# A graph network on one core: the constant rows' matmuls on all 128 partitions instead of three

## The chip, the cores and the metric

The kernel runs on one core of one Trainium2 chip. The metric is the device time of one execution in microseconds; the median of three runs is given. Beside it stands one execution taken by the hardware profiler, from which all the rows and timelines below come. PE is the matmul engine (PEld is its weight load), DVE, ACT and POOL are the vector, scalar and GpSimd engines, SP issues DMAs.

## The reference

Sixteen graphs of 1024 nodes with 128 features each, and a symmetric 0/1 adjacency with ones on the diagonal. A first layer is attention over the neighbours, a second one is three GraphSAGE layers on an adjacency from which some edges are taken first (`_dilate`), and each has a residual. Cut to what matters here:

```
def _sage(x, adj, Wr, Wx, b, mf):
    agg = jnp.einsum('bij,bjd->bid', adj, x) / deg
    out = agg @ Wr + x @ Wx + b
    nrm = jnp.maximum(jnp.linalg.norm(out, axis=-1, keepdims=True), NORM_EPS)
    return out / nrm * mf[..., None]
def _bn(x, g, b):
    ...
    return (x - m) * jax.lax.rsqrt(v + BN_EPS) * g + b
h1 = _bn(jax.nn.relu(_sage(x, adj_d, Wr1, Wx1, b1, mf)), g1, be1)
h2 = _bn(jax.nn.relu(_sage(h1, adj_d, Wr2, Wx2, b2, mf)), g2, be2)
h3 = _bn(jax.nn.relu(_sage(h2, adj_d, Wr3, Wx3, b3, mf)), g3, be3)
xc = jnp.concatenate([h1, h2, h3], axis=-1) * mf[..., None]
return (xc @ Wl + bl) * mf[..., None]
```

The bias `b` of a layer, and what the batch norm of the layer before adds to every node once it is folded into the next weights, are the same row of 128 numbers for all nodes: the constant rows of the title.

## The kernel before

The program has a fast path (`fast`) and a general one behind a flag; the fast path is what runs. It sorts every graph's nodes so that those with many neighbours stand first, and then works in stages, one graph ("batch" below, 16 of them) after the other:

- Attention with the search for the edges to be taken, to about 785 us. It holds no constant row.
- Layer 1, about 790 to 922 us. Per batch, `mix` makes one SAGE product, `turn` transposes the result of the batch before, and beside them run the last part of the edge search (`dil.solve`), the transposes of later batches (`enter`) and the last stores.
- Layer 2, 930 to 1016 us: `mix` and `turn` alone, no DMA.
- Layer 3, 1022 to 1152 us: `mix`, `turn`, and `thirds`, which multiplies the outputs of layers 1 and 2 with their parts of Wl. Results of 11 of the 16 batches are scattered back to the original order of nodes through `y_d` in DRAM and loaded again.
- The final stage, 1162 to 1221 us: `raised` transposes the rows that came back, `final_half` multiplies with the last third of Wl, and the output leaves, for 11 batches by one DMA of SP each, for the other five (`STAY`) by eight scatters of POOL each.

`fast` runs with a manual schedule: each engine executes its instructions in the order in which the program records them. `in_turn` takes one piece at a time of the named generators (a tick), and `clock.later(n, ...)` puts an eviction off by n ticks. In layer 2 the order of a batch is mix, mix, mix, turn, mix, turn: the product with wr and its row; half 1 with wx and its row; half 0 and its row; the transposes of the first half of the batch before; the product with the adjacency; the transposes of the second half. In layer 3 the order is mix, thirds, mix, mix, turn, mix, thirds, turn.

What stands around the matmuls of this change: ACT squares a half (L984) when its row is in, DVE sums the squares (L987), takes the maximum (L1009), ACT the root (L1010), DVE the reciprocal (L1013) and scales both halves (`scale`, L1016). `turn` (L1026) transposes the scaled rows on PE, ACT takes the relu (L1038), DVE the batch norm's sums (L1035). `add` (L1043) is DVE's sum of a PSUM tile and a tile in SBUF. `evict` (L957, L958) is ACT's copy of wr's product, which comes from L946. wx's matmuls are L970, the adjacency's L1006 and L1007, those of `thirds` L1194 and L1195, of `final_half` L1251, and `raised` transposes in L1237.

In layer 3 and after, `pace_scatters` lets POOL issue a scatter (L547) in two of three ticks. Ahead of each, in layer 3, POOL copies a `mark` (L1169) from the newest result of DVE, so that it can't run ahead. A `y` tile has three buffers, so a batch waits for the scatters of an earlier one.

A constant row is added inside the accumulation in PSUM. `pieces` (L615 on) splits the f32 row into three bf16 pieces whose sum is the row, one per partition, and repeats them four times along the free axis; `ones3`, three partitions of 128 ones, is the stationary operand, so that a matmul with three partitions adds the three pieces to all 128 nodes of a tile. These matmuls are:

- `row_of_ph` (L950): 256 columns, 16 times each in layers 2 and 3.
- `row_of` (L975): 512 columns, twice per batch in all three layers, 96 in all.
- in `final` (L1259): 512 columns, 32 times.

In the first batch of layers 2 and 3 (`bias_last`) the three rows come at the end, one after the other, since the row is not ready before.

```
nc.tensor.matmul(halves[g].rearrange("p a b -> p (a b)"), ones3, bias, start=False, stop=(g == 1))
```

Of the kernel before, what the change touches and what calls it, by code (L numbers as in the profile page):

```python
# [8 lines left out]
BF = mybir.dt.bfloat16  # L9
# [6 lines left out]
P = 128  # L16
# [503 lines left out]
def fast(ctx: ExitStack, tc: tile.TileContext, a, out, vp):  # L520
    nc = tc.nc
# [3 lines left out]
    consts = ctx.enter_context(tc.tile_pool(name="consts", bufs=1))  # L525
# [7 lines left out]
    nc.vector.tensor_scalar(identf, jp, 0.0, None, op0=OP.is_equal)  # L533
    eps = consts.tile([P, 1], F32, name="eps")
    nc.vector.memset(eps, EPS)
    ones3 = consts.tile([3, P], BF, name="ones3")
    nc.vector.memset(ones3, 1.0)

    def apart(d, own, *others):

# [71 lines left out]
        while gens:  # L612
            gens = [g for g in gens if _advance(g)]

    def pieces(name, rows, pool):  # L615

        n = len(rows)
        v = pool.tile([3, 2, P], F32, name="pcv", bufs=1)[:, :n]
        part = pool.tile([3, 2, P], BF, name="pcp", bufs=1)[:, :n]
        acc = pool.tile([3, 2, P], F32, name="pca", bufs=1)[:, :n]  # L620
        res = pool.tile([3, n, 4, P], BF, name=name, bufs=1)
        for i, (base, more) in enumerate(rows):
            if base is None:
                nc.vector.tensor_copy(v[:, i, :], more)
            elif more is None:
                nc.vector.tensor_copy(v[:, i, :], base)
            else:
                nc.vector.tensor_add(v[:, i, :], base, more)
        for i in range(3):
            nc.vector.tensor_copy(part, v)  # L630
            if i == 0:
                nc.vector.tensor_scalar(acc, part, identf[:3, i:i + 1], None, op0=OP.mult)
            else:
                nc.vector.scalar_tensor_tensor(acc, part, identf[:3, i:i + 1], acc, op0=OP.mult, op1=OP.add)
            if i < 2:
                nc.vector.tensor_sub(v, v, part)
        nc.vector.tensor_copy(res, acc[:, :, None, :].to_broadcast([3, n, 4, P]))
        return [res[:, i].rearrange("p a b -> p (a b)") for i in range(n)]


    late = ExitStack()
# [5 lines left out]
    rows = ExitStack()  # L647
    with ExitStack() as s1:
# [206 lines left out]
        for i in range(B):  # L855
# [6 lines left out]
            if i == 0:  # L862
# [5 lines left out]
                bs = [rows3(f"b3_{k}", a[f"L1_gnn_b{k}"]) for k in (1, 2, 3)]  # L868
# [23 lines left out]

            return hT, parts()

        bias0, = pieces("pc0", [(bs[0], None)], work)
        ENTER = NB // 2
        H = {}
        for t in range(22):
# [3 lines left out]
            b = t // 4 - 1  # L902
# [36 lines left out]
    def mix(b, hT, wxk, wrk, bias, rbias, ob, on_scalar=False):  # L939

        bias_last = rbias is not None and b == 0
        ph = ps.tile([P, 2, P], F32, name="ph", bufs=ph_bufs)
        for s in range(2):
            nc.tensor.matmul(ph[:, s, :], hT[:, s * P:(s + 1) * P], wrk, start=(s == 0),  # L946
                             stop=(rbias is None and s == 1))

        def row_of_ph():
            nc.tensor.matmul(ph.rearrange("p a b -> p (a b)"), ones3, rbias[:, :2 * P], start=False, stop=True)  # L950

        if rbias is not None and not bias_last:
            row_of_ph()
        hr = work.tile([P, 2, P], F32, name="hr")

        def evict():
            nc.scalar.activation(hr[:, 0, :], ph[:, 0, :], AF.Copy)  # L957
            nc.scalar.activation(hr[:, 1, :], ph[:, 1, :], AF.Copy, scale=kept[:, b, 1:2])  # L958

        if not bias_last:  # L960
            later(1, evict)
            yield
        n = work.tile([P, 4, NB], F32, name="nrm")
        halves = {}

        def wx_half(g):
            po = halves[g] = ps.tile([P, 4, P], F32, name="po", bufs=4)
            for i in range(3, -1, -1):
                c = (4 * g + i) * P
                nc.tensor.matmul(po[:, i, :], hT[:, c:c + P], wxk, start=(i == 3), stop=False)  # L970
            if not bias_last:
                row_of(g)

        def row_of(g):
            nc.tensor.matmul(halves[g].rearrange("p a b -> p (a b)"), ones3, bias, start=False, stop=(g == 1))  # L975

        def squares(g):
            sq = work.tile([P, 4, P], F32, name="sq")
            if on_scalar and g == 1:
                for i in range(4):  # L980
                    later(1 + i // 2, lambda i=i: nc.scalar.activation(
                        sq[:, i, :], halves[g][:, i, :], AF.Square, accum_out=n[:, 0, 4 * g + i:4 * g + i + 1]))
                return
            later(1, lambda: nc.scalar.activation(sq, halves[g], AF.Square))  # L984

            def reduce():
                nc.vector.tensor_reduce(n[:, 0, 4 * g:4 * g + 4], sq, axis=AX.X, op=OP.add)  # L987
                last[0] = n[:, 0, 4 * g:4 * g + 1]

            later(2, reduce)  # L990

        wx_half(1)
        if bias_last:
            wx_half(0)
            row_of_ph()
            row_of(1)
            row_of(0)
            later(1, evict)
            yield
        squares(1)  # L1000
        yield
        if not bias_last:
            wx_half(0)
        yield
        po = halves[0]
        nc.tensor.matmul(po[:, 0, :], accT[:, b, :], hr[:, 0, :], start=False, stop=False)  # L1006
        nc.tensor.matmul(po[:, 1, :], identf, hr[:, 1, :], start=False, stop=True)  # L1007
        squares(0)
        later(2, lambda: nc.vector.tensor_scalar(n[:, 1], n[:, 0], NORM_EPS2, None, op0=OP.max))  # L1009
        later(3, lambda: nc.scalar.activation(n[:, 2], n[:, 1], AF.Sqrt))  # L1010

        def scale():
            nc.vector.reciprocal(n[:, 3], n[:, 2])  # L1013
            for g in (1, 0):
                c = slice(4 * g, 4 * g + 4)
                nc.vector.tensor_mul(ob[:, c, :], halves[g], n[:, 3, c, None].to_broadcast([P, 4, P]))  # L1016

        later(4, scale)
        yield
# [28 lines left out]
    def batchnorm(k, weights):  # L1048

        m = few.tile([P, 8], F32, name=f"bn{k}")  # L1050
        nc.vector.bn_aggr(m[:, 0:2], stats)
        nc.scalar.activation(m[:, 2:3], m[:, 1:2], AF.Sqrt, bias=eps)
        nc.vector.reciprocal(m[:, 3:4], m[:, 2:3])
        nc.vector.tensor_mul(m[:, 4:5], m[:, 3:4], gs[k])
        scaled = []
        for i, w in enumerate(weights):
            t = few.tile([P, P], F32, name=f"ws{i}", bufs=2)
            nc.scalar.activation(t, w, AF.Copy, scale=m[:, 4:5])
            scaled.append(t)
        nc.vector.tensor_mul(m[:, 5:6], m[:, 0:1], m[:, 4:5])  # L1060
        nc.vector.tensor_sub(m[:, 6:7], bes[k], m[:, 5:6])
        t3 = few.tile([P, 3], F32, name=f"t3_{k}")
        nc.vector.tensor_copy(t3, m[:, 6:7].to_broadcast([P, 3]))
        pr = ps.tile([3, 3, P], F32, name="ph")
        for i, w in enumerate(weights):
            nc.tensor.matmul(pr[:, i, :], t3, w, start=(i == 0), stop=(i == len(weights) - 1))
        return scaled, pr
# [62 lines left out]
    with big:  # L1130
        ps = big.enter_context(tc.tile_pool(name="ps", bufs=2, space=PSUM, reuse_waits="tile"))
        r2 = big.enter_context(tc.tile_pool(name="r2", bufs=1, reuse_waits="tile"))
        r2 = [r2.tile([P, 2, N], F32, name=f"r2_{i}") for i in range(B // 2)]
        work = big.enter_context(tc.tile_pool(name="work", bufs=2, reuse_waits="tile"))
        (wxs, wrs, wl0), pr = batchnorm(0, [wx[1], wr[1], wl[:, 0, :]])
        bias, rbias = pieces("pc1", [(bs[1], pr[:, 0, :]), (None, pr[:, 1, :])], few)
        zrow = add_row(bl, pr, 2)
        prev = None
        with tc.tile_pool(name="w2", bufs=2, reuse_waits="tile") as own:
# [31 lines left out]

        with tc.tile_pool(name="w3", bufs=3, reuse_waits="tile") as own:
            (wxs, wrs, wl1), pr = batchnorm(1, [wx[2], wr[2], wl[:, 1, :]])
            bias, rbias = pieces("pc2", [(bs[2], pr[:, 0, :]), (None, pr[:, 1, :])], few)
            zrow = add_row(zrow, pr, 2)
            X2 = {}

# [76 lines left out]
        def final(b, h):  # L1254

            first = [final_half(h, g) for g in range(2)] if b == order[0] else None
            for g in range(2):
                pz = first[g] if first else final_half(h, g)
                nc.tensor.matmul(pz.rearrange("p a b -> p (a b)"), ones3, bias, start=False, stop=True)  # L1259
                half = rows_z(b)[:, 4 * g:4 * g + 4, :]  # L1260
                add(half, half, pz)
                if b in STAY:
                    for k in range(4 * g, 4 * g + 4):
                        waiting.append((ticks3 + 3, lambda k=k: scatter_out(b, k)))
                yield
            if b not in STAY:
                later(2, lambda: apart(nc.sync.dma_start(out[b].rearrange("(k p) d -> p k d", p=P), rows_z(b)), "stores", "out"))
# [13 lines left out]
        drain(raise_next(1))  # L1281
        clock.flush()
        (wl2,), pr = batchnorm(2, [wl[:, 2, :]])
        bias, = pieces("pc3", [(zrow, pr[:, 0, :])], few)
        marked = False
        for i, b in enumerate(order):
            parts = {"final": final(b, hs[b]), "raised": raise_next(i + 1)}
# [589 lines left out]
```

## Time and profile before

| | us |
|---|---|
| median of 3 runs | 1275.23 (1273.57 to 1277.38) |
| span of the profiled execution | 1230.9 |
| outside the span | 44.3 |
| PE busy | 1106.3 (90%) |
| DVE busy | 883.8 (72%) |
| ACT busy | 728.2 (59%) |
| POOL busy | 567.2 (46%) |
| L975, 96 matmuls | 37.0 |
| L1259, 32 matmuls | 12.7 |
| L950, 32 matmuls | 8.9 |

[...] starts are the better measure, and the timeline gives them. [...] Shares of busy time are averages over stages with different limits, so the stages are read apart.

### The profile page before, as it was taken

Reading aid. Unit: us, or ns where it says so; the run is one execution under the profiler, and the core shown is the slowest. Engines: PE = TensorE matmul, PEld = TensorE weight load, DVE = VectorE, ACT = ScalarE, POOL = GpSimd, SP = SyncE. Lnnn points to the kernel's source line nnn. Section 1 sums busy time; section 2 is a strip of 40 time slices with the busy share of each in tenths; the row PEclk is TensorE's granted clock in tenths of the full one; section 3 lists DMA queues with packets and bytes.
Section 4 is the critical chain, followed back from the end, with each engine's and each line's share of the span. In section 5 each row is a group of like instructions: output and inputs, shape, how many; then the busy total and the mean of one; then the engine's idle time right before and its main releaser. Section 6 shows DMA issues by size and latency. Waiting matters only on the chain.

```text
span 1230.9 us, 22315 instructions
## 1 busy us (share of the span) xinstructions
PE 1106.3 (90%) x7787; PEld 824.2 (67%) x7787; DVE 883.8 (72%) x2630; ACT 728.2 (59%) x1570; POOL 567.2 (46%) x1043
## 2 busy tenths in 40 slices
PE   7899999999899899899889888778769979999896
PEld 3566676666576576567567656667657868888775
DVE  6767567579778678778777868688887876666632
ACT  5578788677678678678677752346554543333221
POOL 0330752651743643644535434687410003777775
PEclk8899999999899999999999999889999999999998
DMA  6544244344234344344333410334000012877664
GB/s 209 148 135 138 87 140 153 106 124 150 87 120 152 103 125 155 95 129 139 109 114 106 130 59 27 96 101 115 1 1 1 1 32 78 237 232 214 195 184 134
DMA packets 118146, 143.44 MB, mean 117 GB/s; under 512 B 9212, under 2 KB 94088, under 8 KB 118024
## 3 DMA queue, kind: packets, MB, share of 16 engines
q1 hardware_dynamic: 106120, 110.78, 30.1%
q0 software_dynamic: 11904, 31.15, 7.7%
q8 instruction: 63, 1.03, 0.4%
q14 instruction: 59, 0.48, 0.1%
HBM read 113.39 MB, written 28.51 MB: 115 GB/s over the span
## 4 chain that ended last, share of the span: by engine, by line
PE 56%; DVE 23%; ACT 6%; POOL 6%; issue 4%; DMA 4%; POOLq 0%; DVEq 0%; ACTq 0%; SPq 0%
PE ps L704 10%; PE po L720 10%; PE po L970 6%; PE pm L683 6%; DVE e L707 4%; DMA rows<-in_adj_dram,row 4%; PE pt L1026 3%; PE ph L1194 2%; PE ph L1251 2%; DVE left L312 2%; PE ph L1195 2%; POOL hn L595 2%; PE po L975 2%; ACT e L706 2%; DVE m L369 2%
## 5 line engine op out<-in xcount | busy, mean ns | idle before, releaser
L720 PEld LDWEIGHTS po<-vw,e 128*128 128x128 f32 x2048 | 274.0, 195 | 66.5 <-issue 66.1
L720 PE MATMUL po<-vw,e 128*128 128x129 f32 x2048 | 307.8, 285 | 0.0
L704 PE MATMUL ps<-qT,kT 128*128 128x512 f32 x512 | 273.3, 617 | 0.8 <-ACT e L706 0.8
L707 DVE TENSOR_TENSOR e<-e,ab 128x512 f32<-128x512 f32 x256 | 177.6, 695 | 113.0 <-ACT e L706 111.3
L706 ACT ACTIVATE e<-ps 128x512 f32<-128x512 f32 x256 | 153.0, 598 | 108.2 <-PE ps L704 85.4
L547 POOL DMA_INDIRECT x_d<-xt,slot x128 | 143.6, 1122 | 39.8 <-issue 36.1
L167 ACT ACTIVATE ab<-st,d_one_k 128x1024 bf16<-128x1024 f32 x128 | 146.8, 1147 | 0.0
L583 POOL TENSOR_SCALAR ln_t<-ln_st 128x8 f32<-128x8 f32 x31 | 8.0, 260 | 290.3 <-DVE ln_st L576 233.2
L184 ACT ACTIVATE junk<-st 128x1024 bf16<-128x1024 f32 x112 | 118.2, 1056 | 0.0
L547 POOL DMA_INDIRECT y_d<-y,nodes x88 | 86.5, 983 | 28.9 <-issue 28.3
L729 ACT ACTIVATE o<-po,recips 128x128 f32<-128x128 f32 x128 | 46.8, 368 | 72.4 <-DVE recips L727 72.2
L704 PEld LDWEIGHTS ps<-qT,kT 128*128 128x128 f32 x512 | 79.1, 194 | 8.2 <-issue 3.7
L595 POOL TENSOR_SCALAR hn<-xt,ln 128x128 f32<-128x128 f32 x120 | 76.4, 648 | 1.6
L1038 ACT ACTIVATE r<-pt 128x512 f32<-128x512 f32 x74 | 44.4, 601 | 55.3 <-PE pt L1026 55.3
L984 ACT ACTIVATE sq<-po 128x512 f32<-128x512 f32 x80 | 47.7, 596 | 48.0 <-PE po L975 44.0
L970 PE MATMUL po<-ws,r 128*128 128x128 f32 x512 | 72.8, 286 | 0.0
L1035 DVE BATCH_NORM_STATS2 stats<-r 128x6 f32<-128x512 f32 x74 | 50.8, 687 | 29.2 <-ACT r L1038 29.2
L987 DVE TENSOR_REDUCE nrm<-sq 128x4 f32<-128x512 f32 x80 | 53.9, 676 | 24.6 <-ACT sq L984 23.3
L312 DVE TENSOR_TENSOR_SCAN left<-rows 128x1024 f16<-128x1024 f32 x16 | 38.9, 2432 | 45.1 <-DMA rows<-in_adj_dram,row 45.1
L1169 POOL COPY mark<-y 128x1 f32<-128x1 f32 x30 | 5.8, 192 | 137.1 <-DVE y L1043 134.5
L970 PEld LDWEIGHTS po<-ws,r 128*128 128x128 f32 x512 | 63.0, 194 | 8.6 <-issue 6.8
L199 DVE SCALAR_TENSOR_TENSOR junkv<-pd,ab 128x64 bf16<-128x64 int32 (+7 forms) x128 | 57.8, 451 | 15.1 <-PE pd L193 15.1
(303 smaller groups left out, 2433.2 us busy)
## 6 DMA issues: line engine op xcount, KB each, us to landing
st<-in_adj_dram SPq DMA_DIRECT2D x128, 512.0 KB, 3.7
r<-y_d SPq DMA_DIRECT2D x22, 512.0 KB, 6.5
xt<-x_d SPq DMA_DIRECT2D x16, 524.0 KB, 4.0
xt<-in_x_dram SPq DMA_DIRECT2D x16, 512.0 KB, 4.3
x<-x_d SPq DMA_DIRECT2D x16, 512.0 KB, 4.6
out_dram<-r SPq DMA_DIRECT2D x11, 512.0 KB, 3.3
x_d<-xt,slot POOLq DMA_INDIRECT x128, 2.8
y_d<-y,nodes POOLq DMA_INDIRECT x88, 5.4
```

The lines of the kernel that those rows point to most:

```text
L167: nc.scalar.activation(ab[:, k, :], st, AF.Exp, bias=self.one_k, scale=ONE_K, accum_out=self.deg[:, b, k:k + 1])
L184: nc.scalar.activation(junk(), st, AF.Exp, scale=-ZERO_K, accum_out=zeros)
L199: nc.vector.scalar_tensor_tensor(junk.rearrange("p a b -> p (a b)")[:, :n], pt.rearrange("p a b -> p (a b)").bitcast(I32)[:, :n], 1.0, ab[ ...
L312: nc.vector.tensor_tensor_scan(left[:, ::-1], rows[:, ::-1], rows[:, ::-1], 0.0, op0=OP.add, op1=OP.bypass)
L547: d = nc.gpsimd.indirect_dma_start(out=dst, out_offset=bass.IndirectOffsetOnAxis(ap=slots, axis=0), in_=src, in_offset=None)
L595: engine.tensor_scalar(hn[:, k, :], xt[:, k, :D], minus[:, k // 2, k % 2, None], rstd[:, k // 2, k % 2, None], op0=OP.add, op1=OP.mult)
L683: nc.tensor.matmul(pp, w, hT[:, 512 * g:512 * g + 512], start=True, stop=True)
L704: nc.tensor.matmul(p, K[b][:, k * P:(k + 1) * P], Q[b][:, c], start=True, stop=True)
L706: later(1, lambda: nc.scalar.activation(e, p, AF.Exp))
L707: later(2, lambda: nc.vector.tensor_mul(e, e, AB_[b][:, k, c]))
L720: nc.tensor.matmul(po[:, q % 2, :], E[k][:, i * P:(i + 1) * P], V[b][:, k, :], start=(k == 0), stop=(k == NB - 1))
L970: nc.tensor.matmul(po[:, i, :], hT[:, c:c + P], wxk, start=(i == 3), stop=False)
```

## The change

The stationary operand of ones gets 128 partitions (`full`), and the pieces get 128 partitions too, of which the first three hold the row's pieces as before and the others are zero. The sum is the same. The tiles of pieces are filled with zeros by POOL: the first one ahead of layer 1, the three others together where layer 2 begins. DVE writes the first three partitions as before.

```
-    ones3 = consts.tile([3, P], BF, name="ones3")
-    nc.vector.memset(ones3, 1.0)
+    full = consts.tile([P, P], BF, name="full")
+    nc.vector.memset(full, 1.0)
...
-    def pieces(name, rows, pool):
+    def padded(name, n, pool):
+
+        t = pool.tile([P, n, 4, P], BF, name=name, bufs=1)
+        nc.gpsimd.memset(t, 0.0)
+        return t
+
+    def pieces(tall, rows, pool):
...
-        res = pool.tile([3, n, 4, P], BF, name=name, bufs=1)
...
-        nc.vector.tensor_copy(res, acc[:, :, None, :].to_broadcast([3, n, 4, P]))
-        return [res[:, i].rearrange("p a b -> p (a b)") for i in range(n)]
+        nc.vector.tensor_copy(tall[:3], acc[:, :, None, :].to_broadcast([3, n, 4, P]))
+        return [tall[:, i].rearrange("p a b -> p (a b)") for i in range(n)]
...
-        bias0, = pieces("pc0", [(bs[0], None)], work)
+        bias0, = pieces(padded("pc0", 1, work), [(bs[0], None)], work)
...
-            nc.tensor.matmul(ph.rearrange("p a b -> p (a b)"), ones3, rbias[:, :2 * P], start=False, stop=True)
+            nc.tensor.matmul(ph.rearrange("p a b -> p (a b)"), full, rbias[:, :2 * P], start=False, stop=True)
...
-            nc.tensor.matmul(halves[g].rearrange("p a b -> p (a b)"), ones3, bias, start=False, stop=(g == 1))
+            nc.tensor.matmul(halves[g].rearrange("p a b -> p (a b)"), full, bias, start=False, stop=(g == 1))
...
+        tall_rows = [padded(f"pc{k + 1}", n, few) for k, n in enumerate((2, 2, 1))]
         (wxs, wrs, wl0), pr = batchnorm(0, [wx[1], wr[1], wl[:, 0, :]])
-        bias, rbias = pieces("pc1", [(bs[1], pr[:, 0, :]), (None, pr[:, 1, :])], few)
+        bias, rbias = pieces(tall_rows[0], [(bs[1], pr[:, 0, :]), (None, pr[:, 1, :])], few)
...
-                nc.tensor.matmul(pz.rearrange("p a b -> p (a b)"), ones3, bias, start=False, stop=True)
+                nc.tensor.matmul(pz.rearrange("p a b -> p (a b)"), full, bias, start=False, stop=True)
```

`pieces("pc2", ...)` and `pieces("pc3", ...)` change in the same way. The order of the instructions on PE, DVE, ACT and SP is the same as before; POOL has the four fills more.

More of the change, by code (lines that the diff above doesn't have):

```diff
@@ L1173, in fast @@
             (wxs, wrs, wl1), pr = batchnorm(1, [wx[2], wr[2], wl[:, 1, :]])
-            bias, rbias = pieces("pc2", [(bs[2], pr[:, 0, :]), (None, pr[:, 1, :])], few)
+            bias, rbias = pieces(tall_rows[1], [(bs[2], pr[:, 0, :]), (None, pr[:, 1, :])], few)
             zrow = add_row(zrow, pr, 2)
@@ L1283, in fast @@
         (wl2,), pr = batchnorm(2, [wl[:, 2, :]])
-        bias, = pieces("pc3", [(zrow, pr[:, 0, :])], few)
+        bias, = pieces(tall_rows[2], [(zrow, pr[:, 0, :])], few)
         marked = False
```

## The prediction

> **What bounds the kernel now.** I read the page first (PE 90% busy, no other engine over 72%), then the chain of waits, then busy time by stage, then the timeline around a constant row's matmul, around one batch of layer 2, and on POOL at the end. All 160 such matmuls stand after 790 us: 32 in layer 1, 48 in layer 2, 48 in layer 3, 32 in the final stage; nothing before that changes. Busy time by stage (columns: stretch, length, PE, PEld, DVE, ACT, POOL, clock, DMA share, GB/s; the rows are layer 1, layer 2, layer 3, final):
>
> ```profile
> 785.00:925.00 140.00, 105.92 (x803) 88.83 (x803) 110.16 (x306) 75.94 (x271) 79.96 (x159) 0.91 0.23 62
> 937.00:1003.00 66.00, 65.45 (x462) 52.53 (x461) 53.09 (x106) 36.99 (x93) 0.00 (x0) 1.00 0.00 1
> 1036.00:1147.00 111.00, 111.00 (x874) 98.69 (x873) 72.06 (x132) 39.45 (x92) 81.44 (x140) 1.00 0.74 220
> 1172.00:1221.00 49.00, 48.02 (x324) 37.86 (x324) 19.26 (x28) 11.30 (x20) 36.96 (x39) 0.97 0.59 180
> ```
>
> PE looks like the bound in three of the four. Only layer 3 bears that out, as the last two excerpts below will show. First, what a three-partition matmul costs among full ones (timeline of layer 3, columns: start, length, engine, line):
>
> ```profile
> 1106.91 0.39 PE L970 MATMUL po<-ws,r 128*128 128x128 f32 x2
> 1107.23 0.09 PEld L975 LDWEIGHTS <-ones 3*128 3x128 bf16 x1
> 1107.23 0.38 PE L975 MATMUL po<-pc,ones 3*128 3x512 bf16 x1
> 1107.55 0.41 PEld L970 LDWEIGHTS po<-ws,r 128*128 128x128 f32 x3 [0.23 <-issue]
> 1107.55 0.49 PE L970 MATMUL po<-ws,r 128*128 128x128 f32 x2
> ```
>
> and, from the attention stage, a 16-bit matmul on all 128 partitions among f32 ones:
>
> ```profile
> 123.97 0.86 PEld L327 LDWEIGHTS <-turned 128*128 128x128 f16 x8
> 124.08 1.04 PE L327 MATMUL pd<-onehot,turned 128*128 128x256 f16 x8
> 124.84 0.30 PEld L704 LDWEIGHTS ps<-qT,kT 128*128 128x128 f32 x2
> 124.95 0.59 PE L704 MATMUL ps<-qT,kT 128*128 128x512 f32 x1
> ```
>
> With full partitions the next weights load 0.11 us ahead of their matmul (123.97 against 124.08, 124.84 against 124.95), beside the one that runs; eight 256-column matmuls and the step to f32 take 0.87 us, 0.109 each. With three partitions the load starts with its own matmul (1107.23), 0.21 us after the last f32 start (1107.02, the second of the pair from 1106.91, whose pitch is 0.11), and the next full load waits until 1107.55.
>
> Layer 2, one batch (DVE, then PE's next load):
>
> ```profile
> 956.64 0.69 DVE L1035 BATCH_NORM_STATS2 stats<-r 128x6 f32<-128x512 f32 x1 [0.85 <-ACT r L1038]
> 957.25 0.67 DVE L987 TENSOR_REDUCE nrm<-sq 128x4 f32<-128x512 f32 x1
> 958.04 0.68 DVE L1035 BATCH_NORM_STATS2 stats<-r 128x6 f32<-128x512 f32 x1
> 958.64 0.18 DVE L1013 RECIPROCAL nrm<-nrm 128x8 f32<-128x8 f32 x1
> 958.93 1.29 DVE L1016 TENSOR_TENSOR ob<-po,nrm 128x512 f32<-128x512 f32 x2
> 960.33 0.42 PEld L1026 LDWEIGHTS pt<-identf,ob 128*128 128x128 f32 x4 [0.30 <-issue]
> ```
>
> A loop: the scale (L1016) ends at 960.22, the transposes of its result (L1026) start at 960.33, need 0.6 us, ACT's relu (L1038) another 0.6, and only then DVE's stats start; from 956.64 to 960.22 DVE has no pause. That is 3.58 + 0.11 + 0.6 + 0.6, and with the hand-overs the 5.02 us from one batch to the next. The last constant row before it starts at 959.94; at 0.32 us its successor could have loaded at 960.26, and loads at 960.33. So DVE's loop is already 0.07 us later than PE's own work.
>
> The end, on POOL:
>
> ```profile
> 1155.87 0.98 POOL L547 DMA_INDIRECT y_d<-y,nodes  x1 [0.16 <-issue]
> 1218.31 0.96 POOL L547 DMA_INDIRECT out_dram<-r,nodes  x1 [0.30 <-issue]
> 1219.58 0.96 POOL L547 DMA_INDIRECT out_dram<-r,nodes  x1 [0.30 <-issue]
> 1219.75 0.39 PE L1259 MATMUL ph<-pc,ones 3*128 3x512 bf16 x1
> ```
>
> From 1153.1 on POOL issues 53 scatters (13 to y_d, 40 to out) with no other pause than 0.16 to 0.30: the final stage has two ends at the same time, PE's and POOL's.
>
> **What the Trainium skill says.** "TensorEngine Tiling (Array Packing)", section Tiling Modes: changing the tiling mode drains the engine. The trace agrees in effect: 0.21 and 0.32 us where 0.11 and 0.21 are pitch. "TensorE: Matmul & The Clock Gate", section LDWEIGHTS: loading time follows the columns, not the rows; agrees (91 ns for 3x128, 97 for 128x128 bf16). Same page, Part 1: an idle window of some 3.4 us halves the clock; the trace agrees in that layer 1, where PE is 76% busy, was granted 0.91, and layer 3, where it never rests, 1.00.
>
> **The change part by part.** Each matmul keeps its columns. Removed per constant row: 0.10 ahead of it (0.21 to 0.11), 0.10 behind it (0.32 to 0.215, twice 0.109 for 512 columns), and 0.10 in the next pair of f32 matmuls (0.49 against 0.39 us), so 0.30 us; before transposes the last term is 0.06 (0.66 against 0.60 us for four), so 0.26. PE's whole sum: 72 before f32 matmuls x 0.30 + 75 before transposes x 0.26 + 13 odd ones x 0.2 = 43.7 us. What reaches the end:
>
> Layer 1: DVE leads the chain (L1016, L1035, L369 together 28% of it, L975 3.1%). Walking the chain, 11 constant rows stand in stretches where PE leads, in runs worth 2.6 us; in most, a DVE path is close behind. I take 1.5 (0 to 3).
>
> Layer 2: the loop above holds no constant row. 15 batches gain at most 0.07 each, and I take none of it; 0.3 for the first batch, whose three rows come together. 0.3 (0 to 1.3).
>
> Layer 3: PE starts every instruction at its own pitch, 8.51 us a batch (L950 at 1104.15 and 1112.66), with three rows: 0.30 + 0.30 + 0.26 = 0.86. The next limit is close: thirds' second half ends on PE at 1111.85, DVE adds it from 1111.88 to 1112.57 (L1043), and only then the next thirds may fill that buffer, now at 1112.87. Without 0.30 before it PE would be there at 1112.57, the buffer some 0.1 later. So 0.76 a batch, 15 batches, less some waiting for scatters: 11.2 (7.5 to 12.5). POOL must keep up, since what follows hangs on it: 5.33 scatters a batch (two in three of its eight ticks) at 1.365 (the pitch with no wait, 0.98 + 0.19 for the mark + gaps) is 7.3 us against a new batch of 7.75.
>
> Final: PE's 32 rows are worth 8 us, but POOL's 40 scatters at 1.265 us are not shortened. What is gained is the difference of the two ends: PE's output leaves at 1220.89 and takes 3.3 us (median), POOL's last leaves at 1219.58 and takes 3.7, less with no transfer beside it. 1.5 (0.9 to 2.3).
>
> Added: the square of ones costs DVE the same (memset 165 ns for 3x128 and for 128x128 in the page's groups). The four zero fills go to POOL, at most 1.05 us each (523 ns for 128x512 f32). The first stands between the indirect load issued at 772.22 and work at 777.49, and waits for a transposition and an activation that are over by 768; DVE's copy, which now waits for it, ran at 776.65, so 2.7 us of cover; without it DVE would stall, with the scan L312 and the normalization behind it. The other three fall where POOL waits 134.5 us (for L1169). The first constant row of layer 1 and of the final stage also wait for such a fill, on PE, some 18 us or more after it. Costed at nothing. No DMA is added or moved.
>
> Sum: 1.5 + 0.3 + 11.2 + 1.5 = 14.5 us off the profiled execution: span 1230.9 to 1216.4. The 44.3 us between span and median lie outside it and stay: 1275.2 to 1260.7.
>
> **Rivals.**
> PE bounds all of it: the 43.7 us come in whole, 1231.5. For it: PE's busy shares, and the chain, which in layer 2 and the final stage runs on PE. Against: the 0.07 us and POOL's unbroken row. 0.04.
> Scatters hold layer 3: POOL's pitch there stays near the 1.6 it has (8.51 / 5.33), because landings of 5.5 us or waits on the marks, not PE, set it; then layers 1 to 3 give 1.8, the end 1.5 and layer 3 at most 1: 1271. For it: DMA share 0.74, and y's three buffers wait for scatters. Against: most gaps above 0.16 follow a mark that waited for DVE. 0.14.
> The change doesn't do what it says: the gaps come from separate bf16 loads beside f32, not from partitions: 1275. Against: L327, above. 0.06.
> Slower, by the clock: PE, done sooner, rests more in layers 1 and 2 and falls to half clock more often. One such window of 3.4 us costs a PE-led stretch 1.7; nine more would eat the gain, twelve give 1281. Against: layer 2's new rests are under 1 us each. 0.04.
>
> **Numbers.** Forecast 0.72, with its own costs 1256 to 1266. Adding half-clock windows (one or two either way, 1.7 each) and most of the scatter rival, 1254 to 1270 leaves out about 2 in 10. Within 0.3% (3.8 us, about what this kernel's measurement can tell): the third rival, 0.06. Slower: 0.04. Faster: 0.90.
>
> **What would show it.** Constant rows' starts 0.11 after the matmul before and 0.215 before the next; layer 2 still at 5.0 us a batch, with PE pausing some 0.9 us before the transposes; layer 3 near 7.75; POOL unbroken from layer 3's end, PE done some 6 us before it. Wrong if layer 2 drops under 4.8, layer 3 stays over 8.1, or loads of the square don't overlap.

## The result, and the profile after

The changed kernel takes 1275.09 us in the median of twelve runs (1271.61 to 1280.90), the kernel before 1276.43 in twelve runs on the same chip (1269.89 to 1283.06): ratio 1.000, 95% interval 0.9982 to 1.0018. The forecast was 1260.7 (1254 to 1270).

The profiled run of after took 1274.11 us and its span is 1272.3, so only 1.8 us lie outside the span. For before, 44.3 had been taken to lie there. Busy time by stage in this run (stretch, length, PE, PEld, DVE, ACT, POOL, clock, DMA share, GB/s; layers 1, 2, 3, final):

```profile
806.00:941.00 135.00, 96.70 (x758) 86.84 (x769) 106.96 (x286) 72.18 (x262) 78.72 (x156) 0.90 0.21 58
955.00:1021.00 66.00, 56.02 (x457) 51.09 (x463) 52.54 (x105) 35.76 (x93) 0.00 (x0) 1.00 0.00 1
...
1032.00:1183.00 151.00, 129.26 (x1064) 122.61 (x1081) 93.96 (x179) 47.98 (x116) 93.30 (x160) 0.97 0.63 183
1184.00:1264.00 80.00, 56.75 (x366) 49.78 (x371) 24.83 (x47) 12.96 (x24) 46.45 (x49) 0.84 0.45 140
```

PE, which filled layer 3 of before without a pause, is now idle for some 20 of 151 us there (17 of its matmuls miss a record) and 23 of 80 in the final stage. Yet the matmuls themselves did what was forecast. The timeline of the same run, a constant row of layer 3 (L980 is before's L975, L1031 before's L1026), then a batch of layer 2 (L1021 is L1016), then the end (L1265 is L1259, L1048 is L1043):

```profile
1093.07 0.10 PEld L980 LDWEIGHTS <-full 128*128 128x128 bf16 x1
1093.18 0.38 PE L980 MATMUL po<-pc,full 128*128 128x512 bf16 x1
1093.18 0.57 PEld L1031 LDWEIGHTS pt<-identf,y 128*128 128x128 f32 x4
1093.40 0.60 PE L1031 MATMUL pt<-identf,y 128*128 128x128 f32 x4
...
977.93 1.29 DVE L1021 TENSOR_TENSOR ob<-po,nrm 128x512 f32<-128x512 f32 x2
978.25 0.38 PE L980 MATMUL po<-pc,full 128*128 128x512 bf16 x1
979.37 0.63 PE L1031 MATMUL pt<-identf,ob 128*128 128x128 f32 x4 [0.73 <-DVE ob L1021]
...
1258.07 0.96 POOL L547 DMA_INDIRECT out_dram<-r,nodes  x1 [0.30 <-issue]
1264.13 0.69 DVE L1048 TENSOR_TENSOR r<-r,ph 128x512 f32<-128x512 f32 x1 [2.06 <-PE ph L1265]
```

The square's load starts 0.11 us before its matmul, the next load beside the matmul, and the next matmul 0.22 after it, where before had 0.21 and 0.32. The first steady batches of layer 3 took 7.7 to 7.8 us, as forecast, but the later ones 8.6 to 10.4. At the end PE and DVE are not done before POOL's last scatter, but 6.1 us after it.

What PE waits for is seen at one hand-over of layer 3, from the second half of `thirds` on PE (L1201) to DVE's sum (L1048) and back to PE (L1200), and then in the final stage:

```profile
1087.22 0.39 PE L1201 MATMUL ph<-ws,r 128*128 128x128 f32 x2
1087.45 0.60 PE L1031 MATMUL pt<-identf,y 128*128 128x128 f32 x4
1088.33 0.27 PE L955 MATMUL ph<-pc,full 128*128 128x256 bf16 x1
1088.55 0.69 DVE L1048 TENSOR_TENSOR r<-x,ph 128x512 f32<-128x512 f32 x1 [1.03 <-PE pt L1031]
1089.29 0.49 PE L1200 MATMUL ph<-ws,r 128*128 128x128 f32 x2 [0.69 <-DVE r L1048]
1089.31 0.58 ACT L1043 ACTIVATE pt<-pt 128x512 f32<-128x512 f32 x1 [1.49 <-PE ph L955]
...
1206.37 0.63 PE L1243 MATMUL pt<-identf,r 128*128 128x128 f32 x4
1208.58 1.28 DVE L1048 TENSOR_TENSOR r<-r,ph 128x512 f32<-128x512 f32 x2 [3.62 <-remote]
1208.69 1.09 ACT L1248 ACTIVATE hT<-pt 128x512 f32<-128x512 f32 x2 [2.40 <-remote]
1209.32 1.16 PE L1257 MATMUL ph<-ws,r 128*128 128x128 f32 x8 [2.32 <-DVE r L1048]
```

The last matmul of L1201 starts at 1087.34 and is over by 1087.61; DVE is free from 1087.52 and needs nothing else (its wait names PE's semaphore alone), and yet it starts at 1088.55. That semaphore was updated at 1088.53. The transposes end at 1088.05, and ACT starts on them at 1089.31. So by the profile PE's work was done, and its signal came 0.9 and 1.25 us late. Ends of matmuls are modelled in the profile, though, so whether the signal alone was late, or PE's last writes too, it can't tell. ("remote" stands where the profile finds no instruction that ended the wait.) From 1207.0 to 1208.55 every engine stands still, until two sums and two activations go at once: four signals of PE, 1.8 to 3.6 us old by the ends of their matmuls, arrived within 0.22 us (the semaphore's records are at 1208.55, .61, .71 and .77). The same hand-over in the changed kernel on another chip, to compare:

```profile
1060.04 0.39 PE L1201 MATMUL ph<-ws,r 128*128 128x128 f32 x2
1060.26 0.60 PE L1031 MATMUL pt<-identf,y 128*128 128x128 f32 x4
1060.46 0.69 DVE L1048 TENSOR_TENSOR r<-x,ph 128x512 f32<-128x512 f32 x1
...
1061.14 0.27 PE L955 MATMUL ph<-pc,full 128*128 128x256 bf16 x1
1061.25 0.33 PE L1200 MATMUL ph<-ws,r 128*128 128x128 f32 x1
```

Here DVE starts 0.03 us after the matmul's end, and PE goes from its constant row to L1200 without a pause.

### The profile page after: what moved, and what is told of

Read it like the earlier page. It is cut to its first block, busy times and chain, and to the rows that moved or that the text cites. A ratio compares the mean times of both kernels' runs of the same rounds, so it can differ in the third digit from the quotient of the medians.

```text
span 1272.3 us, 22275 instructions
## 1 busy us (share of the span) xinstructions
PE 1082.3 (85%) x7743; PEld 828.9 (65%) x7787; DVE 885.5 (70%) x2630; ACT 723.8 (57%) x1570; POOL 570.4 (45%) x1047
## 4 chain that ended last, share of the span: by engine, by line
PE 48%; DVE 27%; ACT 7%; issue 5%; POOL 5%; DMA 4%; another core or an unknown queue 2%; DVEq 0%; POOLq 0%; ACTq 0%; SPq 0%
PE ps L709 10%; PE po L725 9%; PE pm L688 6%; DVE e L712 4%; DMA rows<-in_adj_dram,row 3%; PE po L975 3%; DVE stats L1040 3%; DVE ob L1021 3%; PE ph L1200 2%; PE ph L1257 2%; PE pt L1031 2%; DVE left L312 2%; ACT e L711 2%; POOL hn L595 2%
## 5 line engine op out<-in xcount | busy, mean ns | idle before, releaser
L1043 ACT ACTIVATE r<-pt 128x512 f32<-128x512 f32 x74 | 44.3, 601 | 56.3 <-PE pt L1031 51.7
L975 PE MATMUL po<-ws,r 128*128 128x128 f32 x512 | 69.5, 281 | 1.2
L992 DVE TENSOR_REDUCE nrm<-sq 128x4 f32<-128x512 f32 x80 | 54.0, 676 | 22.1 <-ACT sq L989 11.4
L199 DVE SCALAR_TENSOR_TENSOR junkv<-pd,ab 128x64 bf16<-128x64 int32 (+7 forms) x128 | 57.8, 452 | 15.2 <-PE pd L193 11.4
L975 PEld LDWEIGHTS po<-ws,r 128*128 128x128 f32 x512 | 66.8, 198 | 1.3
```

## The experiments

They ran on five chips. On four of them (e0 with e1, e2, e3, e4) the kernel before takes 1228 to 1229 us in the median, on the one of e5 1265.6; in the result it took 1276.4. Below, "a chip of the 1228 kind" or "of the 1276 kind" (that of e5 is counted among these) says only what it showed at that time. Each ratio is to the kernel before on the same chip.

**The two kernels again.**

> The kernel before, profiled again on the same chip as the next three, because its first profiled execution (span 1230.9 us) is 43 us under the median of its timed runs, while the first profile of the changed kernel (span 1272.3) agrees with its own. Theory A (the first profile was of an unusually short execution; usually transfers in layer 3 and the final stage end last): span 1265 to 1280, layer 3 over 8.7 us a batch instead of 8.51 and over 25 us between the last product of layer 3 and the first relu of the final stage or spread over the final stage. Theory B (the first profile was typical in its stages, and the change itself slowed layer 3 and the final stage): layer 3 at 8.5 us a batch again, final stage about 55 us, and the difference lies elsewhere.

> The changed kernel, profiled again on the same chip as the kernel before. Both theories: constant rows start 0.11 us after the matmul before and the next 0.216 us after them. Theory A: same span as the kernel before within 6 us, layer 3 between 8.0 and 9.5 us a batch with DVE's additions (thirds) waiting for loads or scatters. Theory B: layer 3 and the final stage together over 15 us longer than in the kernel before.

> The changed kernel again, timed. A chip with before at 1276: 1270 to 1280, ratio 0.997 to 1.003, layer 3 at 8.6 us a batch and a final stage of about 80. A chip with before at 1228: 1213 to 1217, ratio 0.988 to 0.991, 7.72 a batch and a final stage of 52.

> The changed kernel, with more rounds for a narrower interval. Chip with before at 1228: ratio 0.987 to 0.990, so 12 to 16 us. Chip with before at 1276: 0.997 to 1.003.

e0: before 1228.19 us (1224.04 to 1233.87); a single profiled run took 1225.09 with before and 1214.64 with after. e2: after 1212.91 (1208.73 to 1218.91), before 1228.97, ratio 0.9884 (0.9824 to 0.9945). e4: after 1215.67 (1212.42 to 1220.26), before 1228.39, ratio 0.9900 (0.9878 to 0.9923). On the chips of e2 and e4 the change brings 16 and 13 us; 14.5 were forecast. The stages of their profiles, from the instruction that opens each (the first copy of wr's product, then each layer's batch norm) to the next:

| us | start | layer 1 | layer 2 | layer 3 | rest | span |
|---|---|---|---|---|---|---|
| before, first profile | 791.1 | 131.0 | 91.8 | 145.5 | 71.5 | 1230.9 |
| e0, e2, e4 before | 786.8, 790.9, 786.2 | 128.1, 128.2, 130.8 | 91.2, 91.2, 91.7 | 145.5 each | 71.7, 71.3, 71.8 | 1223.3, 1227.1, 1225.9 |
| e0, e2, e4 after | 788.8, 789.8, 789.6 | 128.2, 127.4, 130.6 | 91.8, 91.7, 91.1 | 133.6 each | 70.3, 70.2, 70.3 | 1212.8, 1212.8, 1215.2 |
| e5 before | 807.4 | 123.8 | 91.7 | 145.9 | 90.5 | 1259.4 |
| after, the result | 806.2 | 134.8 | 91.2 | 151.0 | 89.1 | 1272.3 |
| e5, after with both repairs (more room, faster pace) | 807.5 | 125.8 | 91.0 | 152.3 | 88.1 | 1264.7 |

The first profile of before has the stages of the second row, so it counts to the 1228 kind.

**Without the round trip through DRAM in layer 3.** In both kernels the scatters to `y_d` and the loads of it are left out, so the last third multiplies rows in the wrong order.

```
-                if b >= 3:
-                    later(3, lambda b=b: load_back(b - 3))
-                if b not in STAY:
-                    scatter_rows(b, y)
-            for b in range(B - 3, B):
-                load_back(b)
```

> Kernel before without the way of 11 batches through y_d: layer 3 neither scatters its rows nor loads them back, so the final stage works on rows in the wrong order; all else stays. Theory A (these transfers end last in layer 3 and delay the final stage): 20 to 45 us shorter than the kernel before, layer 3 at PE's own 8.51 us a batch. Theory B: 5 to 18 us shorter, the tail of scatters after layer 3 alone.

> The same edit in the changed kernel. Theory A: without these transfers the freed PE time comes through in layer 3, 7.75 us a batch against 8.51, so 9 to 13 us shorter than the same edit of the kernel before. Theory B (a chain of DVE and ACT takes over in layer 3 as in layer 2): within 3 us of the same edit of the kernel before.

Before 1228.57 us, ratio 1.0010 (0.9988 to 1.0032); after 1217.07, ratio 0.9902 (0.9868 to 0.9936). Nothing is gained by leaving 88 scatters and 22 loads out, where both theories had expected a gain in before, and layer 3 takes 145.5 and 133.6 as with them. The end hardly comes sooner in the changed kernel either, since POOL's 40 scatters to the output begin 10.2 us into the rest without these transfers and 11.4 with them (e4). So on this chip scatters don't hold layer 3, and the idea that these transfers are what makes a run take 1276 found no support; that chip was not of that kind, so it wasn't refuted there either.

**More room between PE and those who wait for it.**

```
-  in_turn(["mix", "thirds", "mix", "mix", "turn", "mix", "thirds", "turn"], parts, pace_scatters)
+  in_turn(["mix", "mix", "thirds", "mix", "turn", "mix", "thirds", "turn"], parts, pace_scatters)
...
-            pz = ps.tile([P, 4, P], F32, name="ph")          # final_half
+            pz = ps.tile([P, 4, P], F32, name="po", bufs=4)
```

> The kernel before again, for a profile beside the others. Two kinds of chip have been seen: before at about 1276 us (where after was no faster) and before at about 1228 (where after took some 13 less). Theory A, late signals: on a chip of the first kind PE's completion signals reach DVE and ACT 0.9 to 5 us late where DMAs run (in the profile of after from the result 26 late hand-overs of 33 us in layer 3, 8 of 21 us in the final stage, none in layer 2). Then this profile shows the same there: a batch of layer 3 at 8.9 to 9.5 us, a final stage of 70 to 85 us, layer 2 at 91 to 92. Theory B, the loads and scatters themselves take longer on such a chip: then waits for DMAs, not for PE, grow. On a chip of the second kind: span 1222 to 1232, layer 3 at 8.51 a batch, no hand-over from PE more than 0.5 late after 785 us.

> Before with more room between PE and those who wait for its signals: in layer 3 the first half of thirds comes after half 1 with wx, 1.3 us later, and in the final stage PE's products go to the four PSUM buffers of po instead of two. Theory A, on a chip with before at 1276: 10 to 30 us shorter, since a late signal no longer stops PE. Theory B: within 3 us of before. On a chip with before at 1228 both say within 3 us (PE has no pause in layer 3; POOL holds the final stage).

> The same room in the changed kernel. Theory A, on a chip with before at 1276: 20 to 40 us shorter than before and 8 to 15 shorter than the kernel before with the same room, as the change's own gain comes back. Theory B: within 3 us of after. On a chip with before at 1228: 1212 to 1216, up to 2 us under after (7.65 instead of 7.72 a batch in layer 3).

This chip was of the 1228 kind. Before with room: 1228.18 us, ratio 0.9992 (0.9974 to 1.0010). After with room: 1215.56, ratio 0.9914 (0.9880 to 0.9948), no different from after; its layer 3 went from 133.6 to 132.6, 0.06 us a batch (7.72 to 7.66), which is what the buffer of `thirds` had held PE for: 8.51 less the 0.86 named for three constant rows is 7.65.

**A sum that is put off.** In `thirds`, DVE's sum of the second half waits for an activation of the same tile, as a late signal from PE would make it.

```
+  nc.scalar.activation(hop, more, AF.Copy, scale=0.0)
+  nc.vector.scalar_tensor_tensor(z, more, hop[:, 0, 0:1], first, op0=OP.add, op1=OP.add)
```

> Before, with DVE's sum of the second half of thirds put off: it waits for an activation of the same tile by ACT (0.58 us and two hand-overs, 0.64 in all), as a late signal from PE would put it off. A. The next first half of thirds must wait for that sum; in before 1.4 us of PE's work lie between, of which signal, sum and hand-overs take 1.06, so 0.34 are spare: 0.3 of the 0.64 reach PE, 8.8 instead of 8.51 us a batch, 4 to 5 us longer than before in all. Rival: the sum has more time than that or PE finds other work, and before stays within 2 us.

> The same delay in the changed kernel. A: here only 1.1 us of PE's work lie between and nothing is spare (7.72 a batch), so the 0.64 come in whole: 8.35 a batch, 9 to 10 us longer than after, and 5 us less is left of the change's gain: 4 to 10 us under before at 1228. So a late signal of that size takes a third of the gain, not all of it. Rival: the gain goes altogether (within 3 us of before with the delay), as on the result's chip; then delay alone explains that result.

Before 1236.64 us, ratio 1.0068 (1.0045 to 1.0090); after 1223.90, ratio 0.9933 (0.9908 to 0.9958). A steady batch of layer 3 goes from 8.51 to 8.96 in before and from 7.72 to 8.41 in after. After, in the timeline:

```profile
1072.43 0.60 ACT L1212 ACTIVATE hop<-ph 128x512 f32<-128x512 f32 x1 [1.15 <-PE ph L1201]
1073.06 0.75 DVE L1213 SCALAR_TENSOR_TENSOR y<-ph,hop,x 128x512 f32<-128x512 f32 x1 [0.75 <-ACT hop L1212]
1073.87 0.49 PE L1200 MATMUL ph<-ws,r 128*128 128x128 f32 x2 [0.48 <-DVE y L1213]
```

The delay of 0.64 us reaches PE whole in after (0.69 a batch) and to two thirds in before (0.45; 0.3 had been expected, and 4 to 5 us in all where 7.2 came), so the gain of a batch shrinks from 0.79 to 0.55 us. Layer 3 keeps 9.2 us of its 11.9 (153.6 against 144.4), and 12.7 lie between the two medians. A delay of this one size in both kernels doesn't take the gain away: the rival fell. Longer delays were not tried.

**POOL's row at the end.** In e3 the eight scatters of graph 5 to the output are left out, in e4 the last eight, those of graph 14.

```
-                if b in STAY:
+                if b in STAY and b != 5:      # e4: b != 14
```

> Before without eight of POOL's 40 scatters to the output (the rows of graph 5 aren't written). Theory: PE and POOL end the final stage together in before (PE's last sum at 1216.5, POOL's last scatter at 1215.8), so that 10 us less for POOL (8 x 1.265) bring at most 1 to 3 us: 1225 to 1229 on a chip with before at 1228. Rival: POOL alone holds that stage already in before: 1218 to 1220. (On a chip with before at 1276 this kernel shows what before does there in layers 1 to 3.)

> The same in the changed kernel, where PE's last sum is at 1195.0 and POOL's last scatter at 1203.2. Theory: POOL's unbroken row hides PE's gain of the final stage, so here it comes out: 6 to 9 us under after, 1204 to 1208, and 18 to 22 under the kernel before without these scatters. Rival: something else holds the end (the landing of the stores): within 3 us of after.

> The changed kernel without the last eight of POOL's 40 scatters to the output (the rows of graph 14 aren't written) instead of eight in the middle. Theory: POOL's row holds the end, and so its last scatter goes from 1203.2 to 1193.1 and PE's last sum at 1195.0, with a store by SP behind it, becomes the end: 5 to 8 us under after, 1205 to 1208 where after is at 1213. Rival: the landing of the stores by SP holds it: within 2 us of after.

e3: before 1226.96 us, ratio 0.9984 (0.9968 to 1.0000); after 1210.62, ratio 0.9833 (0.9814 to 0.9853), 2 to 5 under after on the chips of e2 and e4 (on this one it wasn't run), where 6 to 9 were expected. In that profile POOL, with less to do, runs dry and waits 6.35 us for the sums of graph 8, so its last scatter moves by only 4.7 us, and the span by 4.4. e4, without the last eight: 1205.83, ratio 0.9833 (0.9809 to 0.9857), 9.8 us under after on the same chip (5 to 8 were expected). After, and then without the last eight:

```profile
1197.31 0.69 DVE L1048 TENSOR_TENSOR r<-r,ph 128x512 f32<-128x512 f32 x1 [0.42 <-PE ph L1265]
1198.02 0.96 POOL L547 DMA_INDIRECT out_dram<-r,nodes  x1 [0.31 <-issue]
...
1205.61 0.96 POOL L547 DMA_INDIRECT out_dram<-r,nodes  x1 [0.31 <-issue]
```

```profile
1191.93 0.96 POOL L547 DMA_INDIRECT out_dram<-r,nodes  x1 [0.31 <-issue]
...
1193.84 0.69 DVE L1048 TENSOR_TENSOR r<-r,ph 128x512 f32<-128x512 f32 x1 [0.42 <-PE ph L1265]
```

In after DVE's last sum is 8.3 us before POOL's last scatter; take eight scatters away, and the sum is the end. So POOL's unbroken row does hide what PE saves in the final stage on these chips.

**A faster pace for POOL, and both repairs together.**

```
-            if ticks3 % 3 and waiting and waiting[0][0] <= ticks3:
+            if ticks3 % 4 and waiting and waiting[0][0] <= ticks3:
```

> The kernel before once more, for a profile, in case the chip is of the kind where before takes 1276. There: theory A1, each late signal is an added delay: layer 3 at 8.9 to 9.1 us a batch, half a us above the 8.6 of after in the result. Theory A2, PE's signals go through a path that passes only so many, whatever PE's own pace: layer 3 at the same 8.6 to 9.0 as after, with late hand-overs there too. On a chip with before at 1228: 1222 to 1232 and 8.51 a batch.

> The changed kernel with a scatter in three of four ticks instead of two of three: six per batch of layer 3, 6 x 1.365 = 8.2 us against a batch of 7.72. If POOL keeps up to its own limit of 7.72 / 1.365 = 5.65 per batch, some 5 of the 13 scatters that are left at the end of layer 3 are gone by then, and POOL ends 4 to 6 us sooner: 1207 to 1211 where after is at 1213. Rival: POOL, saturated, makes y's buffers late, and layer 3 grows over 7.8 a batch: 1213 to 1225.

> The kernel before a last time, with a profile. If the chip takes 1276 for it: A1, layer 3 at 8.9 to 9.1 us a batch; A2, 8.6 to 9.0 and hand-overs from PE up to 5 us late, as in the profile of after from the result. If it takes 1228: 1222 to 1232, 8.51 a batch.

> The changed kernel with both repairs: the first half of thirds after half 1 with wx (the buffer has 1.3 us more time), PE's final products in the four buffers of po, and a scatter in three of four ticks. On a chip with before at 1228, theory (POOL is the end of it all, from its first scatter at 1024 to its last: 88 x 1.365 + 40 x 1.265 = 171 us, 5 less than the 176 it takes with the new pace): 1208 to 1214, no more than 5 us under after. Rival: PE's layer 3 and final stage set the end, and the freed buffers bring 5 us and more: under 1208. On a chip with before at 1276: A1 and A2 both 1240 to 1265 if the late signals are what holds after there, since four buffers bridge them in the final stage.

e4: 1214.55 us, ratio 0.9893 (0.9866 to 0.9919), not told apart from after (1215.67); POOL needs 176.4 us from its first scatter (1024.1) to its last (1200.5) where after needs 177.5 (1028.1 to 1205.6), so it was near its limit already. Of the 4 to 6 us expected nothing is seen, nor did layer 3 grow, as the rival had it (7.72 a batch). e5 came to a chip where before takes 1265.62 (1259.10 to 1272.70). There after with both repairs takes 1271.30 (1261.77 to 1283.97), ratio 1.0035 (1.0016 to 1.0053): slower than before. 1240 to 1265 had been expected. The changed kernel without the repairs wasn't run on this chip. Busy time in layer 3 and in the rest, first before at 1228, then after at 1228, then before and after with both repairs on the chip of e5:

```profile
1010.00:1156.00 146.00, 139.36 (x1084) 123.34 (x1085) 94.77 (x180) 49.49 (x117) 93.84 (x161) 0.98 0.64 191
1156.00:1216.00 60.00, 56.31 (x373) 44.34 (x372) 25.62 (x47) 13.51 (x24) 45.51 (x49) 0.94 0.59 179
```

```profile
1009.00:1142.50 133.50, 127.44 (x1081) 122.81 (x1082) 94.27 (x178) 48.70 (x116) 93.31 (x160) 0.97 0.70 207
1142.50:1195.00 52.50, 49.31 (x377) 45.11 (x375) 26.18 (x49) 13.61 (x24) 40.11 (x43) 0.91 0.64 197
```

```profile
1023.00:1169.00 146.00, 139.75 (x1083) 123.44 (x1084) 94.32 (x179) 49.27 (x117) 93.72 (x160) 0.98 0.64 190
1169.00:1251.00 82.00, 64.05 (x374) 49.33 (x374) 25.17 (x47) 13.16 (x24) 46.33 (x50) 0.85 0.44 136
```

```profile
1024.00:1176.00 152.00, 135.09 (x1078) 128.53 (x1078) 92.99 (x179) 47.60 (x116) 92.88 (x159) 0.93 0.62 182
1177.00:1256.00 79.00, 59.10 (x374) 51.34 (x373) 24.95 (x48) 13.39 (x24) 46.52 (x50) 0.80 0.44 136
```

Before's layer 3 is the same on both kinds of chip, 8.51 us a batch and now and then 8.63. What follows layer 3 is not: 19 us longer (90.5 against 71.3), with PE's signals late there too (before on the chip of e5):

```profile
1203.86 0.66 PE L1237 MATMUL pt<-identf,r 128*128 128x128 f32 x4
1206.45 1.29 DVE L1043 TENSOR_TENSOR r<-r,ph 128x512 f32<-128x512 f32 x2 [5.00 <-remote]
1206.56 1.09 ACT L1242 ACTIVATE hT<-pt 128x512 f32<-128x512 f32 x2 [3.78 <-remote]
1207.19 2.07 PE L1251 MATMUL ph<-ws,r 128*128 128x128 f32 x8 [2.67 <-DVE r L1043]
```

In the changed kernel with both repairs, signals are late in layer 3 too. Of 14 batches eight take 7.66 or 7.67 us, as with more room on the 1228 kind; the other six take 8.2 to 15.1. The one between 1061 and 1075 takes 13.6, and after its pauses PE runs at half clock (f32 matmuls 0.21 us apart instead of 0.11, from 1066.4 to 1069.7). The four buffers of the final stage only let four sums arrive at once:

```profile
1207.26 2.48 DVE L1048 TENSOR_TENSOR r<-r,po 128x512 f32<-128x512 f32 x4 [7.79 <-PE po L1265]
```

In this profile PE itself pauses too, where it waits for nothing that the profile shows: inside one product with wx in layer 3, and inside products of the final stage. The matmuls shown carry no wait.

```profile
1062.60 0.62 PE L975 MATMUL po<-ws,r 128*128 128x128 f32 x4 [0.84 <-issue]
1064.05 0.77 PE L975 MATMUL po<-ws,r 128*128 128x128 f32 x2 [0.84 <-issue]
...
1218.87 0.37 PE L1257 MATMUL po<-ws,hT 128*128 128x128 f32 x1 [0.24 <-issue]
1219.58 0.36 PE L1257 MATMUL po<-ws,hT 128*128 128x128 f32 x1 [0.34 <-issue]
1220.28 0.37 PE L1257 MATMUL po<-ws,hT 128*128 128x128 f32 x1 [0.34 <-issue]
```

From 1218.2 on these matmuls start 0.7 or 1.4 us apart instead of 0.11. So more room for those who wait for PE could not help there: PE was held up too, by what is not known. The profile of before on this chip has no such pause in layer 3 or after it, that of the result one, of 0.5 us.

I compared each hand-over from PE to DVE or ACT with the same one in a profile from a 1228 chip, and counted those that came over 0.3 us later. A hand-over is the time from the end of PE's matmul, or of the waiting engine's own previous instruction if that is later, to the start of the one that waited. In layer 3: before 13, 7.5 us in sum, the longest 0.8; after in the result 27, 32.8 us, longest 2.6; with both repairs 31, 45.2 us, longest 4.5. Behind layer 3 all three have 16 or 17, of 42 to 62 us, and ahead of layer 2, the attention included, 17 to 20, of 29 to 33 us. In layer 2, which has no DMA: none in the three. Of hand-overs from DVE, ACT and POOL: one in the three, of 0.8 us. Profiles of one kernel from two 1228 chips, compared in the same way, have none at all. Late hand-overs overlap, so their sums are not time lost.

The transfers themselves are no longer there: packets of SP's queue fill 29.6% of 1259.4 us in before on the chip of e5 and 30.3% of 1223.3 in e0, those of POOL's queue 7.6% and 7.8%. So the theory of e2 that loads and scatters take longer on such a chip finds no support.

Both theories of e4 and e5 fell in part. That each late signal adds the same delay to either kernel (A1) asks for 8.9 to 9.1 us a batch in before, and it has 8.5. That PE's signals pass only at a set pace (A2) asks for late hand-overs up to 5 us in before's layer 3, and the longest is 0.8. That layer 3 takes about as long (145.9, 151.0, 152.3) however fast PE could go looks like what is left of A2; but the eight batches of 7.66 speak against a set pace over the whole layer.

## Why the prediction was wrong

**Two steps failed.** The first is "The 44.3 us between span and median lie outside it and stay". They lie inside. The profile has the stages of the 1228 kind, the median is of the 1276 kind; each run has its span 1.8 us under its time (1225.9 for 1227.68 in e4, 1272.3 for 1274.11 in the result). Between e2's profile of before and e5's, 32.3 us come in at these places: start +16.5, layer 1 -4.4, layer 2 +0.5, layer 3 +0.4, rest +19.2. So the sum of 14.5 was made for executions with another balance than those that were timed. That alone would not have cost the gain: half of the 32.3 us come before layer 1, where nothing was changed, and layer 3 of before is the same on both kinds.

The second is the term of layer 3, 11.2 us. It took the hand-over from PE to DVE's sum and on to the next `thirds` as the profile showed it, "the buffer some 0.1 later", and put late hand-overs at nothing. On the chip of the result DVE's sum started 0.9 to 2.6 us after PE's last matmul instead of 0.03, PE waited for the buffer, and most batches took 8.6 to 10.4 us where 7.75 were named.

**The constant row** (0.30 less each before f32 matmuls, 0.26 before transposes): right, as the batch of 7.66 us with room shows.

**Layer 1** (1.5) and **layer 2** (0.3): no run changes these two, so all 17 profiles on 1228 chips count, 8 of before and 9 of after. Their medians go from 128.2 to 128.9 and from 91.7 to 91.1 us, while profiles of one kernel differ by 3.2 and 0.8. So layer 1 shows no gain, and that of layer 2 is not told from its first batch, which takes 1.8 to 3.0 us in either kernel. The 5.02 us of layer 2 stayed, with PE pausing 0.73 us where 0.9 were named. Layer 1 of the result's profile is 11 us longer than that of before on the chip of e5 (134.8 against 123.8), more than layer 3's difference; no run tells the chip from the change there.

**Layer 3** (11.2): 11.9 on 1228 chips, 7.72 us a batch against the 7.75 named, so the mechanism was right there and not by luck. On the chip of the result this term turned into a loss: 151.0 us, where before has 145.9 on the chip of e5 (two chips, one profile each). On one chip, e5's, it is 152.3 against 145.9 with the repairs in. In the result's profile the loss is PE waiting for sums and buffers whose signals came late, at a clock of 0.97, as in e2's after. With both repairs the pauses of PE itself and the half clock after them (0.93) come to it.

**Final stage** (1.5): 1.4 on 1228 chips, and for the reason given, POOL's row. On the other kind POOL isn't the end at all; it waits for sums that came late, in both kernels (rest 90.5 before, 89.1 after).

**The rivals.** That scatters hold layer 3 fell with e1, on a 1228 chip. That the gaps come from bf16 loads fell with the timeline; its time, 1275, came out by luck, from another cause. Of the slower case, the clock, a part is seen: layer 3 with both repairs was granted 0.93 on the chip of e5, in two batches whose half clock begins after PE had paused. The risk that decided, two kinds of chip, was not among the rivals, though the 44.3 us pointed to it.

**What stays open.** Why PE's hand-overs are late at some times or on some chips (e5 and the result), in the stages with DMAs alone, and why more so in layer 3 of the changed kernel than of before. PE without pauses can't be the whole answer, since before has none in layer 3 either. That the signals alone are late is not shown, since PE itself pauses too in one of the profiles. On no chip of the 1276 kind were before and the plain changed kernel both profiled, so the loss in layer 3 is put together from two chips, or from one with the repairs in. Undoing the change for layer 3 alone, or fewer transfers, was not tried on such a chip.

## What to carry to other kernels

Hold the span of the profile against the time of the runs first. Here they differ by 1.8 us within one run; a gap of 44.3 meant that the profile showed another balance than the one that was timed, and a forecast made on it needs a case of its own for that. A saving on the busiest engine is worth its sum only while those who wait for its signals get them in time. Look at how much work lies between an instruction and the reuse of its buffer (1.1 us here, 1.4 before). A matmul on three partitions among full ones costs 0.3 us more than the same on 128 with zeros, which is worth removing wherever PE sets the pace.

## What the runs showed of the hardware that was not expected

- The same program takes 1228 to 1229 us on four chips, and 1266 and 1276 us in e5 and in the result. Single instructions last as long on both kinds (DVE's sum 0.69 us, f32 matmuls 0.11 apart); time is lost in hand-overs from PE, and in one profile in pauses of PE itself and half clock after them.
- DVE and ACT can start up to 5 us late (9 with both repairs) on what PE has done by the profile, with four of PE's signals arriving within 0.22 us, while hand-overs from DVE and ACT are on time.
- PE can start matmuls that wait for nothing 0.7 or 1.4 us apart instead of 0.11 (e5 with both repairs, six times in a row).
- On such chips the profile also holds a quarter fewer records of semaphore updates (10,477 in e5 against 13,942 in e2, both before), so that waits are named by what happened to come last ("remote", or an instruction long done). Whether the missing records and the late signals have one cause, no run shows.
